# One transfer of 96 rows on partitions 16 to 111, in place of two of 48 rows on partitions 0 to 95

## The chip, the cores and the metric

The kernel runs on one core of one Trainium2 chip. The metric is the device time of one execution in microseconds. The kernel before takes 3562.27 us (median of three runs, 3552.61 to 3563.42). The profile that is read below is of one more execution, which took 3547.51 us.

## The reference, cut to what matters

The input x has one image, 48 channels and 256 x 256 pixels in 32-bit floats (12.58 MB). Two layers follow one another, each adding its result to its input.

```python
# group norm: 16 groups of 3 channels, mean and variance over the whole image
x = x + conv_attention(gn(x))     # layer 0
x = x + window_mix(gn(x))         # layer 1

def conv_attention(x):            # w_qkv (144,48), w_dw (144,1,3,3), w_proj (48,48)
    qkv = dwconv3x3(einsum('bchw,oc->bohw', x, w_qkv), w_dw)
    q, k, v = heads(unfold(split(qkv)))     # 8 heads, 4x4 patches, padded by one border of patches
    attn = softmax(einsum('bhcn,bhcm->bhnm', l2norm(q), l2norm(k)) * temperature)
    return einsum('bchw,oc->bohw', fold(einsum('bhcn,bhnm->bhcm', v, attn)), w_proj)

def window_mix(x):                # 64 x 64 windows, three terms
    return einsum('bcphqw,twW,thH,tcC->bCpHqW', windows(x), Ws, Hs, Cs)
```

The change touches the first group norm, the output projection `w_proj` with the residual that follows it, and the second group norm.

## The kernel before, in words

The image is handled as two halves of 128 rows. A tile that holds "both halves" has 96 partitions: the 48 channels of the upper half on partitions 0 to 47, the 48 channels of the lower half on partitions 48 to 95. So one matmul with a block-diagonal weight (`wq`, `wp`) works on both halves. DRAM keeps x as channel, row, column, and each half of a tile is brought in by a transfer of its own with 48 rows.

**Constants** (L84 to L131). Small weights are loaded from GpSimd's queue (POOL), one after another: `tb` (L89), the group matrix `gm` (L91), twelve pieces of weights into `wq`, `wr` and `wp` (L104, L108), and 21 pieces of the depthwise weights into `dwt` (L114). That makes 35 transfers. [...]the ninth waits until the first has landed, and so on.

**First norm** (L417 to L446). POOL clears a small tile `zr` (L421), whose rows serve as the zero rows above and below an intermediate image in DRAM (L424). x is read whole into `xr`, ten blocks of rows, the upper half from SyncE's queue (SP) and the lower from ScalarE's (L432). VectorE (DVE) takes statistics of two rows at a time (`bn_stats`, L436, 64 of them), joins them (`bn_aggr`, L133), and `group_stats` forms each group's mean and 1/std by two matmuls with `gm`. The result scales `wq` and `wr`, and a copy of `wr` goes to partitions 64 to 111 by a transfer (L441).

**Pointwise and depthwise stages, attention**. From the resident `xr` TensorE forms q, k, v of the first two heads (L155), and the depthwise filter of the first head follows (`depthwise_first`). The attention over eight heads (L674 and on, an order written out by hand) takes most of the time. Its last head also loads the first three tiles `xt0` to `xt2` of x (L756, 24 transfers of 192 KB) for the residual, and stores its results to `os_` in DRAM (L645). `os_` has 16 blocks of 256 patches; `store` puts patches of the upper half into blocks 0 to 7, those of the lower half into blocks 8 to 15.

**Projection and residual** (L787 to L828). Eight steps. Each brings 96 rows of attention results (`pot`, two transfers of 768 KB, L798) and, from the fourth step on, 96 rows of x (`pxt`, the same size, L800), both with three buffers; TensorE multiplies by `wp` (16 matmuls, L812), DVE adds onto the x tile (four adds, L819) and takes statistics (eight, L823), and POOL stores the tile to `x1s` in DRAM (two transfers, L828). SP also brings the first pieces of the next stage (`lxq`, L785). Then the second norm is finished by a chain of small steps (L133 to L149, L863 to L876), and the last stage (L941 to L1002) reads `x1s`.

Except in blocks marked `manual_schedule`, the order on each engine comes from the framework's planner: it takes, of the instructions that it holds to be ready, the one that was written first.

Of the kernel before, what the change touches and what calls it, by code (L numbers as in the profile page):

```python
# [9 lines left out]
F32 = mybir.dt.float32  # L10
F32R = mybir.dt.float32r
AF = mybir.ActivationFunctionType
# [5 lines left out]
C = 48  # L18
H = W = 256
HALF = H // 2  # L20
P2 = 2 * C
KS = 4
KK = KS * KS
NH = 8
HD = C * KK // NH
NT = (H // KS) * (W // KS)
NBORDER = (H // KS + 2) * (W // KS + 2) - NT
EPS = 1e-5
# [8 lines left out]
M0 = H0 * HC  # L37
# [4 lines left out]
TP = 256  # L42
# [5 lines left out]
def conv_preact_kernel(  # L48
# [15 lines left out]
    nc = tc.nc  # L64
    xc = x.rearrange("b c y x -> (b c) y x")
    oc = out.rearrange("b c y x -> (b c) y x")

    const = ctx.enter_context(tc.tile_pool(name="const", bufs=1))
# [11 lines left out]
    os_ = dram.tile([NT // TP, C * KK, TP], F32, name="os_")  # L80
    x1s = dram.tile([C, H, W], F32, name="x1s")


    ident = const.tile([128, 128], F32, name="ident")  # L84
    make_identity(nc, ident)
    ones = const.tile([C, 128], F32, name="ones")
# [3 lines left out]
    gm = const.tile([P2, P2], F32, name="gm")  # L90
    nc.gpsimd.dma_start(out=gm, in_=gmat)  # L91
# [3 lines left out]
    wq = const.tile([P2, 2 * M0], F32, name="wq")  # L95
    nc.vector.memset(wq, 0.0)
    wr = const.tile([64 + C, M1], F32, name="wr")
    wp = const.tile([P2, P2], F32, name="wp")
    nc.vector.memset(wp, 0.0)
    for s in range(2):  # L100
        r = slice(s * C, (s + 1) * C)
        for h in range(NH if s == 0 else H0):
            o = s * M0 + h * HC if h < H0 else (h - H0) * HC
            nc.gpsimd.dma_start(  # L104
                out=(wq[r] if h < H0 else wr[0:C])[:, o : o + HC].rearrange("c (z e) -> c z e", z=3),
                in_=w_qkvT.rearrange("c (z h e) -> h c z e", z=3, h=NH)[h],
            )
        nc.gpsimd.dma_start(out=wp[r, r], in_=w_projT)  # L108
    dwt = const.tile([NP1, NH, 9], F32, name="dwt")
    dws = w_dw.rearrange("(z h e) i a b -> z e h (i a b)", z=3, h=NH)  # L110
    for z in range(3):
        for j in range(CH):
            p = (z * CH + j) * 6
# [3 lines left out]

    mean0 = const.tile([P2, 1], F32, name="mean0")
    rstd0 = const.tile([P2, 1], F32, name="rstd0")
    mean1 = const.tile([P2, 1], F32, name="mean1")  # L120
    rstd1 = const.tile([P2, 1], F32, name="rstd1")
# [8 lines left out]
    def group_stats(st, mean, rstd, pool, pspool, behind=lambda: None):  # L130

        mv = pool.tile([P2, 2], F32, name="mv")
        nc.vector.bn_aggr(mv, st.rearrange("p n s -> p (n s)"))  # L133
        pm = pspool.tile([P2, 1], F32, name="pm", tag="pstat")
        nc.tensor.matmul(pm, lhsT=gm, rhs=mv[:, 0:1], start=True, stop=True)
        behind()
        nc.vector.tensor_copy(mean, pm)
        d = pool.tile([P2, 1], F32, name="gsd")
        nc.vector.tensor_sub(d, mv[:, 0:1], mean)
        e = pool.tile([P2, 1], F32, name="gse")  # L140
        nc.vector.scalar_tensor_tensor(e, d, d, mv[:, 1:2], ALU.mult, ALU.add)
        pv = pspool.tile([P2, 1], F32, name="pv", tag="pstat")
        nc.tensor.matmul(pv, lhsT=gm, rhs=e, start=True, stop=True)
        behind()
        f = pool.tile([P2, 1], F32, name="gsf")
        nc.vector.tensor_scalar_add(f, pv, EPS)
        g = pool.tile([P2, 1], F32, name="gsg")
        nc.scalar.activation(g, f, AF.Sqrt)  # L148
        nc.vector.reciprocal(rstd, g)  # L149
        return mv, e  # L150
# [166 lines left out]
    NM = NT // 512  # L317
# [99 lines left out]
    with tc.tile_pool(name="xn", bufs=1) as xnp, tc.tile_pool(name="cst", bufs=1) as cst, tc.tile_pool(  # L417
# [7 lines left out]
        xr = xnp.tile([P2, HALF, W], F32, name="xr")  # L425
        parts = [16] * 7 + [8, 4, 4]
        st0 = cst.tile([P2, HALF * W // 512, 6], F32, name="st0")
        for i, LR in enumerate(parts):
            j = sum(parts[:i])
            for s in range(2):  # L430
                eng = nc.sync if s == 0 else nc.scalar
                eng.dma_start(  # L432
                    out=xr[s * C : (s + 1) * C, j : j + LR, :], in_=xc[:, s * HALF + j : s * HALF + j + LR, :]
                )
            for i in range(0, LR, 2):
                nc.vector.bn_stats(st0[:, (j + i) // 2, :], xr[:, j + i : j + i + 2, :].rearrange("p a b -> p (a b)"))  # L436
        group_stats(st0, mean0, rstd0, cst, nps)

        nc.vector.tensor_scalar_mul(wq, wq, rstd0)
        nc.vector.tensor_scalar_mul(wr[0:C], wr[0:C], rstd0[0:C])  # L440
        nc.gpsimd.dma_start(out=wr[64 : 64 + C], in_=wr[0:C])  # L441
        for g, (w, k) in enumerate(((wq, P2), (wr, C))):
            m = w.shape[1]
            pb = nps.tile([128, 1], F32, name="pb0", tag="pstat")
            nc.tensor.matmul(pb[:m], lhsT=w[:k], rhs=mean0[:k], start=True, stop=True)
            nc.vector.tensor_scalar_mul(bias[:m, g : g + 1], pb[:m], -1.0)  # L446
# [31 lines left out]
        for i in range(NH + 1):  # L478
            nc.tensor.matmul(pr[:, i : i + 1], lhsT=row[:, i, :], rhs=ones[0:1, 0:1], start=True, stop=True)
# [63 lines left out]
    with tc.tile_pool(name="ahead", bufs=2) as ah, tc.tile_pool(name="ae", bufs=3) as ae, tc.tile_pool(  # L543
# [94 lines left out]
        def store(h, pair):  # L638

            T = 512 // TP  # L640
            for u in range(2):
                m, last, j = parts_of(2 * pair + u)
                for p0, p1, n, c in ((0, HD, m, 0), (HD, 128, last, j * 32)):
                    rows = os_[n * T : (n + 1) * T, h * HD + c : h * HD + c + p1 - p0, :]
                    nc.gpsimd.dma_start(  # L645
                        out=rows.rearrange("t c n -> c t n"),
                        in_=oaccs[h, pair][p0:p1, u, :].rearrange("c (t n) -> c t n", t=T),
                    )
# [14 lines left out]
        with tc.manual_schedule():  # L663
            load_query(0, 1)
            block = scores(0, 0)
            for h in range(NH):
                more = h + 1 < NH
                rows = {r: Depthwise(h + 1, r) for r in range(CR + 1)} if more else {}
                for g in range(NG):
                    p, d, n = rows.get(g - 2), rows.get(g - 1), rows.get(g)  # L670

                    if not more and g == 0:
                        convolution.close()
                        early = ExitStack()  # L674
                        pe = early.enter_context(tc.tile_pool(name="pe", bufs=1, side="right"))
                        xts = [pe.tile([P2, RP, W], F32, name=f"xt{t}") for t in range(NX)]
# [55 lines left out]
                    for k in range(NK):  # L732
# [18 lines left out]
                        if not more and 0 < g <= 2 * NX and k in (1, 3):  # L751
                            i = (g - 1) * 2 + k // 2
                            t, y = i // 4, i % 4 * (RP // 4)
                            for half in range(2):
                                y0 = half * HALF + t * RP + y
                                nc.sync.dma_start(  # L756
                                    out=xts[t][half * C : (half + 1) * C, y : y + RP // 4, :],
                                    in_=xc[:, y0 : y0 + RP // 4, :],
                                )
# [27 lines left out]
    with tc.tile_pool(name="pj", bufs=3) as pj, tc.tile_pool(name="pjs", bufs=1) as pjs, tc.tile_pool(  # L787
        name="pps", bufs=3, space=PSUM
    ) as pps, tc.tile_pool(name="pp1", bufs=1, space=PSUM) as pp1:
        st1 = pjs.tile([P2, HALF * W // 512, 6], F32, name="st1")  # L790
        ov = os_.rearrange("t (c k) n -> t c k n", k=KK)
        for t in range(HALF // RP):
            ot = pj.tile([P2, KK, NP], F32, name="pot")
            xt = xts[t] if t < NX else pj.tile([P2, RP, W], F32, name="pxt")
            for s in range(2):
                r = slice(s * C, (s + 1) * C)
                y0 = s * HALF + t * RP
                nc.sync.dma_start(out=ot[r], in_=ov[s * (NT // 2 // TP) + t])  # L798
                if t >= NX:
                    nc.sync.dma_start(out=xt[r], in_=xc[:, y0 : y0 + RP, :])  # L800
# [3 lines left out]
            for part in range(np):  # L804
# [3 lines left out]
                for ki in range(KS):  # L808
                    ps = pps.tile([P2, KS, n], F32, name="pps")
# [16 lines left out]
                for s in range(2):  # L826
                    y0 = s * HALF + t * RP + ys.start
                    nc.gpsimd.dma_start(out=x1s[:, y0 : y0 + R, :], in_=xt[s * C : (s + 1) * C, ys])  # L828
# [10 lines left out]
        at = pjs.tile([C, 64 + CK], F32, name="at")  # L839
# [3 lines left out]
        gm2 = pjs.tile([P2, 64 + CK], F32, name="gm2")  # L843
        nc.vector.memset(gm2, 0.0)
        for o in (0, 64):
            nc.vector.tensor_copy(gm2[:, o : o + C], gm[:, 0:C])
        busy = pps.tile([P2, KS, 128], F32, name="pps")

        def occupy(rhs):

            n = rhs.free_size()
            nc.tensor.matmul(  # L852
                busy.rearrange("p k n -> p (k n)")[:, :n], lhsT=ident[: rhs.shape[0], :P2], rhs=rhs, start=True, stop=True
            )

        with tc.manual_schedule(engines={mybir.EngineType.PE}):
# [5 lines left out]
            pc1 = pp1.tile([64 + CK, 1], F32, name="pc1", tag="pstat")  # L862
            nc.tensor.matmul(pc1, lhsT=gm2, rhs=e1, start=True, stop=True)  # L863
            occupy(nmx)
            rstd2 = pjs.tile([64 + CK, 1], F32, name="rstd2")
# [4 lines left out]
            nc.vector.tensor_scalar_mul(csn[: 64 + CK], csn[: 64 + CK], rstd2)  # L870
            mcol = pjs.tile([C, 64 + CK], F32, name="mcol")
            nc.vector.tensor_scalar_mul(mcol, at, mean1[0:C])
            pb1 = pp1.tile([64 + CK, T3 * C], F32, name="pb1")
            nc.tensor.matmul(pb1, lhsT=mcol, rhs=csn[0:C], start=True, stop=True)  # L874
# [200 lines left out]
```

## Time and profile before

| | us |
|---|---|
| profiled execution, its own time | 3547.51 |
| its span (first to last instruction) | 3545.7 |
| median of three runs | 3562.27 |
| x load and first norm, to the first pointwise matmul | 0 to 72.7 |
| pointwise matmuls | 72.7 to 131.7 |
| depthwise stage and attention, to the last weighing matmul | 131.7 to 3161.5 |
| projection, from its first load to the joining of statistics | 3165.5 to 3300.8 |
| end of the second norm | 3307.5 |
| last stage | 3307.8 to the end |

The span is the time from the first to the last instruction of one execution. Engines are PE (TensorE), DVE (VectorE), ACT (ScalarE), POOL (GpSimd) and SP (SyncE). A timeline row has start, duration, engine, line, operation and tiles, and in brackets the idle time before it and what ended that. A row of groups has the total busy time, the mean of one in ns, then the idle time before them and what ended it. A row of stretches has, for each engine, busy time and number of instructions; then the TensorE clock granted, the busy share of the 16 DMA engines and their rate.

### The profile page before, as it was taken

The numbers are of one execution on the slowest core, as the hardware profiler recorded it, in microseconds if no ns is written. First come the engines' busy times: TensorE is split into PE (matmuls) and PEld (weight loads), VectorE is DVE, ScalarE is ACT, GpSimd is POOL, SyncE is SP. The second block draws the span as 40 slices with busy tenths as digits, with TensorE's granted clock in tenths as the row PEclk, the third lists the DMA queues.
The fourth block names the chain that finished last, engine by engine and source line by source line (L and its number), as shares of the span: only waits on it lengthen the run. The fifth ranks groups of instructions, "written<-read, shape, count | busy, mean of one in ns | idle before, by whom it ended". The sixth has DMA issues, their size and how long they took to land. (4 is left out here: it accounts for less than half of the span.)

```text
span 3545.7 us, 63152 instructions
## 1 busy us (share of the span) xinstructions
PE 3339.1 (94%) x25836; PEld 1859.1 (52%) x25836; DVE 1990.7 (56%) x2983; ACT 1900.0 (54%) x2890; POOL 562.6 (16%) x648
## 2 busy tenths in 40 slices
PE   2878999999999999999999999999999999985898
PEld 1334455555555555555555555555555555531576
DVE  5463675168726872687268727862786222238543
ACT  0245677557645664666467646764676444420343
POOL 2030112012201220122012211221122100000123
PEclk9998999999999999999999999999999999997999
DMA  7455666633332333333233323332333221039764
GB/s 161 165 116 155 164 171 170 178 108 93 83 84 84 95 90 79 86 96 92 78 87 95 88 79 86 96 88 78 85 94 93 75 54 37 19 73 281 204 168 108
DMA packets 229730, 384.13 MB, mean 108 GB/s; under 512 B 77058, under 2 KB 174706, under 8 KB 224920
## 3 DMA queue, kind: packets, MB, share of 16 engines
q1 hardware_dynamic: 191158, 264.95, 27.4%
q0 software_dynamic: 34784, 106.40, 13.3%
q10 hardware_dynamic: 3490, 8.64, 1.1%
q8 instruction: 207, 3.39, 0.4%
q14 instruction: 91, 0.75, 0.1%
HBM read 234.76 MB, written 144.90 MB: 107 GB/s over the span
## 5 line engine op out<-in xcount | busy, mean ns | idle before, releaser
L588 ACT ACTIVATE e<-big,nmx 128x1024 f32<-128x1024 f32 x1024 | 1144.7, 1118 | 907.0 <-PE big L351 889.1
L351 PE MATMUL big<-kt,qt 128*128 128x512 f32 x6144 | 1457.3, 394 | 31.2 <-DMA kt<-qkv 26.2
L622 PE MATMUL big<-e,vn 128*32 128x512 f32 x12288 | 1348.4, 593 | 1.0 <-DVE vn L606 1.0
L351 PEld LDWEIGHTS big<-kt,qt 128*128 128x128 f32 x6144 | 1141.3, 188 | 370.8 <-issue 121.1
L636 DVE TENSOR_TENSOR oacc<-big,oacc 128x1024 f32<-128x1024 f32 x359 | 438.3, 1221 | 760.8 <-PE big L622 760.8
L622 PEld LDWEIGHTS big<-e,vn 128*32 128x32 f32 x12288 | 384.5, 110 | 881.9 <-issue 815.8
L239 DVE SCALAR_TENSOR_TENSOR acc<-pad,dwt,acc 126x1024 f32<-126x1024 f32 x592 | 765.6, 1293 | 33.8 <-ACT acc L220 18.1
L309 POOL DMA_DIRECT2D qkv<-o x72 | 53.0, 737 | 1331.9 <-ACT o L293 1331.9
L303 POOL TENSOR_TENSOR ol<-o,oh 126x1024 fp32r<-126x1024 f32 x78 | 185.3, 2376 | 271.6 <-DVE ss L254 198.6
L602 DVE TENSOR_REDUCE zt<-zs 128x1 f32<-128x5 f32 x256 | 38.7, 151 | 327.1 <-ACT e L588 291.3
L588 ACT ACTIVATION_READ_ACCUMULATOR e<-big,nmx 128x1 f32 x1024 | 196.0, 191 | 0.0
L293 ACT COPY o<-acc 126x1024 f32<-126x1024 f32 x74 | 161.6, 2184 | 0.0
L812 PE MATMUL pps<-pot,wp 96*96 96x512 f32 x128 | 77.0, 765 | 58.7 <-DMA pot<-os__70 46.0
L972 ACT COPY lyt<-pb 128x1024 f32<-128x1024 f32 x69 | 69.9, 1012 | 111.0 <-PE pb L965 108.4
L191 ACT ACTIVATE ot<-big,bias 108x1024 f32<-108x1024 f32 x64 | 68.1, 1112 | 105.8 <-PE big L184 68.5
L220 ACT ACTIVATE acc<-pad,dwt 126x1024 f32<-126x1024 f32 x74 | 84.0, 1135 | 75.9 <-DMA pad<-t 67.8
L148 ACT ACT_TABLE_LOAD x2 | 2.6, 1283 | 204.5 <-DMA x1s<-pxt 153.2
L250 ACT ACTIVATE sq<-acc 126x1024 f32<-126x1024 f32 x74 | 78.4, 1059 | 60.0 <-DVE acc L239 49.1
L228 PE MATMUL dps<-pad,diag 126*126 126x512 f32 x216 | 96.0, 604 | 15.4 <-DMA pad<-t 15.4
L325 POOL DMA_DIRECT2D kt<-qkv x44 | 23.0, 543 | 516.5 <-PE big L351 504.3
L951 DVE COPY lzt<-pa 128x864 f32<-128x864 f32 (+1 forms) x69 | 67.4, 1000 | 59.7 <-PE pa L941 59.7
L254 DVE TENSOR_REDUCE ss<-sq 126x64 f32<-126x1024 f32 x80 | 97.3, 1218 | 6.2 <-ACT sq L250 6.2
(142 smaller groups left out, 1964.5 us busy)
## 6 DMA issues: line engine op xcount, KB each, us to landing
pad<-t SPq DMA_DIRECT2D x238, 254.0 KB
t<-ot SPq DMA_DIRECT2D x64, 435.4 KB
qkv<-ol POOLq DMA_DIRECT2D x78, 336.0 KB, 6.5
qkv<-oh POOLq DMA_DIRECT2D x70, 336.0 KB, 5.7
qt<-qkv SPq DMA_DIRECT2D x176, 96.0 KB
xs<-in_x_dram SPq DMA_DIRECT2D x64, 192.0 KB
pot<-os__70 SPq DMA_DIRECT2D x16, 768.0 KB
out_dram<-lrt POOLq DMA_DIRECT2D x96, 128.0 KB, 3.8
```

Source lines behind the costliest of these rows:

```text
L220: nc.scalar.mul(self.acc, self.pad[:, 0:KS, 0:W], dwt[:, self.h, 0:1])
L228: nc.tensor.matmul(ps[:, i, :], lhsT=diag[:, tap, :], rhs=self.pad[:, y : y + 2, dx : dx + W], start=(tap == 0), stop=(tap == 8),)
L239: nc.vector.scalar_tensor_tensor(self.acc, self.pad[:, dy : dy + KS, dx : dx + W], dwt[:, self.h, tap : tap + 1], self.acc, ALU.mult, ALU.add,
L250: nc.scalar.activation(self.sq, self.acc, AF.Square)
L254: nc.vector.tensor_reduce(self.ss, self.sq.rearrange("p a (x b) -> p x a b", b=KS), AX.XY, ALU.add)
L293: nc.scalar.copy(self.o.rearrange("p (a b) x -> p a b x", a=KS), self.acc.rearrange("p a (x b) -> p a b x", b=KS))
L303: eng.tensor_sub(self.ol, self.o, self.oh.bitcast(F32))
L351: nc.tensor.matmul(ps[:, i, :], lhsT=qt[:, r, q0 : q0 + 128], rhs=kts[2 * j + i][:, r // 2, :], start=(r == 0), stop=(r == 2),)
L588: nc.scalar.activation(e[:, j * 1024 : (j + 1) * 1024], ps.rearrange("p a b -> p (a b)"), AF.Exp, bias=nmx[:, b : b + 1], accum_out=zs[:, ...
L622: nc.tensor.matmul(ps[p * 32 : (p + 1) * 32, u, :], lhsT=vn[:, c * 32 : (c + 1) * 32], rhs=e[:, n * 512 : (n + 1) * 512], start=(i == 0), ...
L636: nc.vector.tensor_add(oaccs[h, pair], ps, old)
L812: nc.tensor.matmul(ps[:, i : i + step, :], lhsT=wp, rhs=ot[:, ki * KS + i : ki * KS + i + step, part * n : (part + 1) * n], start=True, st ...
```

## The change

The tiles of the two halves get 112 partitions. Partition 16 + 2c + s holds channel c of half s; partitions 0 to 15 hold zeros. As x is stored channel, row, column, the rows "channel, half" are then evenly spaced in DRAM, and one transfer brings all 96. This holds for `xr`, `xt`, `pot`, `pxt` and the stores to `x1s`; the blocks of `os_` are renumbered so that the two halves of one step are neighbours.

The zeros are written by ScalarE in `xr` (ten copies of a zero from `zr`, one for each block of rows), and by POOL in the other tiles (nine clearings of 16 partitions by 4096 values: three in the last head, six at the start of the projection; `pot` and `pxt` become six tiles that are used in turn).

Weights and constants follow: `gm`, `wq`, `wp` are laid out for the new order (two small transfers for the group matrix in place of one, and copies on DVE), `gm2` moves to the start, the copy of `wr` to partitions 64 to 111 is made before the norm and both copies are scaled after it, for which two more small matmuls (`pc0`) and a second square root stand behind the first norm. The second norm gets one more small matmul (`pd1`).

```diff
+OFF = 16
+PF = OFF + P2
+    xh = x.rearrange("b c (s y) x -> (b c s) y x", s=2)
...
-    gm = const.tile([P2, P2], F32, name="gm")
-    nc.gpsimd.dma_start(out=gm, in_=gmat)
+    gm = const.tile([PF, PF], F32, name="gm")
...
+    for s in range(2):
+        nc.gpsimd.dma_start(
+            out=gt[OFF + s :: 2], in_=gmat.rearrange("(u c) (v d) -> u c v d", u=2, v=2)[s]
+        )
+    nc.vector.tensor_copy(gm[:, OFF:].rearrange("p (c s) -> p s c", s=2), gt)
...
-        nc.gpsimd.dma_start(out=wp[r, r], in_=w_projT)
+        nc.gpsimd.dma_start(out=wt[OFF + s * C : OFF + (s + 1) * C, s], in_=w_projT)
+    nc.gpsimd.dma_start(out=wr[64 : 64 + C], in_=wr[0:C])
+    nc.vector.tensor_copy(wp[:, OFF:].rearrange("p (c s) -> p s c", s=2), wt)
...
+        hole = zr[:OFF, 0:1].rearrange("p (u v) -> p u v", u=1)
         for i, LR in enumerate(parts):
             j = sum(parts[:i])
-            for s in range(2):
-                eng = nc.sync if s == 0 else nc.scalar
-                eng.dma_start(
-                    out=xr[s * C : (s + 1) * C, j : j + LR, :], in_=xc[:, s * HALF + j : s * HALF + j + LR, :]
-                )
+            nc.scalar.copy(xr[:OFF, j : j + LR, :], hole.to_broadcast([OFF, LR, W]))
+            nc.sync.dma_start(out=xr[OFF:, j : j + LR, :], in_=xh[:, j : j + LR, :])
...
+        nc.tensor.matmul(pc0, lhsT=gm2, rhs=mv0[:, 0:1], start=True, stop=True)
+        nc.vector.tensor_copy(means, pc0)
...
+        nc.tensor.matmul(pc0, lhsT=gm2, rhs=e0, start=True, stop=True)
+        nc.vector.tensor_scalar_add(rstds, pc0, EPS)
+        nc.scalar.activation(rstds, rstds, AF.Sqrt)
+        nc.vector.reciprocal(rstds, rstds)
 
         nc.vector.tensor_scalar_mul(wq, wq, rstd0)
-        nc.vector.tensor_scalar_mul(wr[0:C], wr[0:C], rstd0[0:C])
-        nc.gpsimd.dma_start(out=wr[64 : 64 + C], in_=wr[0:C])
+        for o in (0, 64):
+            nc.vector.tensor_scalar_mul(wr[o : o + C], wr[o : o + C], rstds[o : o + C])
...
+                    n, v = n % (NM // 2), n // (NM // 2)
+                    rows = os_.rearrange("(t v) c n -> v t c n", v=2)[v]
...
+                        for t in xts:
+                            nc.gpsimd.memset(t[:OFF], 0.0)
...
-                            for half in range(2):
-                                y0 = half * HALF + t * RP + y
-                                nc.sync.dma_start(
-                                    out=xts[t][half * C : (half + 1) * C, y : y + RP // 4, :],
-                                    in_=xc[:, y0 : y0 + RP // 4, :],
-                                )
+                            y0 = t * RP + y
+                            nc.sync.dma_start(
+                                out=xts[t][OFF:, y : y + RP // 4, :], in_=xh[:, y0 : y0 + RP // 4, :]
+                            )
...
+        pots = [pj.tile([PF, KK, NP], F32, name=f"pot{t}") for t in range(3)]
+        xus = xts + [pj.tile([PF, RP, W], F32, name=f"pxt{t}") for t in range(3)]
+        for t in pots + xus[NX:]:
+            nc.gpsimd.memset(t[:OFF], 0.0)
         for t in range(HALF // RP):
-            ot = pj.tile([P2, KK, NP], F32, name="pot")
-            xt = xts[t] if t < NX else pj.tile([P2, RP, W], F32, name="pxt")
-            for s in range(2):
-                r = slice(s * C, (s + 1) * C)
-                y0 = s * HALF + t * RP
-                nc.sync.dma_start(out=ot[r], in_=ov[s * (NT // 2 // TP) + t])
-                if t >= NX:
-                    nc.sync.dma_start(out=xt[r], in_=xc[:, y0 : y0 + RP, :])
+            ot = pots[t % 3]
+            xt = xus[t if t < NX else NX + (t - NX) % 3]
+            nc.sync.dma_start(out=ot[OFF:], in_=ov[t])
+            if t >= NX:
+                nc.sync.dma_start(out=xt[OFF:], in_=xh[:, t * RP : (t + 1) * RP, :])
...
-                for s in range(2):
-                    y0 = s * HALF + t * RP + ys.start
-                    nc.gpsimd.dma_start(out=x1s[:, y0 : y0 + R, :], in_=xt[s * C : (s + 1) * C, ys])
+                y0 = t * RP + ys.start
+                nc.gpsimd.dma_start(out=x1h[:, y0 : y0 + R, :], in_=xt[OFF:, ys])
...
+            nc.tensor.matmul(pd1, lhsT=gm2, rhs=mv1[:, 0:1], start=True, stop=True)
+            mcol = pjs.tile([64 + C, 64 + CK], F32, name="mcol")
+            nc.vector.tensor_scalar_mul(mcol, at, pd1)
```

## The prediction

> **What bounds the kernel now.** I read the page first, its busy times and slices.
>
> ```profile
> PE 3339.1 (94%) x25836; PEld 1859.1 (52%) x25836; DVE 1990.7 (56%) x2983; ACT 1900.0 (54%) x2890; POOL 562.6 (16%) x648
> ...
> DMA  7455666633332333333233323332333221039764
> GB/s 161 165 116 155 164 171 170 178 108 93 83 84 84 95 90 79 86 96 92 78 87 95 88 79 86 96 88 78 85 94 93 75 54 37 19 73 281 204 168 108
> ```
>
> TensorE is busy nearly all the time, except in the first slice and in slices 35 to 37: the load of x with the first norm, and the projection. The change works in these two; in the attention between them the tiles of x are loaded under matmuls. So I asked for stretches of both stages, the timeline of POOL and DVE, DVE's waits in the projection, and groups that give prices. The stretches:
>
> ```profile
> 6.00:55.00 49.00, 4.77 (x20) 4.40 (x20) 30.03 (x65) 1.28 (x1) 6.63 (x12) 1.00 1.00 205
> ...
> 3166.00:3198.00 32.00, 15.67 (x30) 5.70 (x31) 16.44 (x18) 0.00 (x0) 1.90 (x7) 0.71 1.02 187
> 3198.00:3240.00 42.00, 30.33 (x51) 9.90 (x49) 39.47 (x38) 0.00 (x0) 3.02 (x6) 0.74 1.00 299
> 3240.00:3300.00 60.00, 33.78 (x52) 11.16 (x53) 43.99 (x49) 0.00 (x0) 5.03 (x10) 0.67 1.00 279
> ```
>
> In all four the DMA share (last but one) is full, while the rate (last) differs: 205 GB/s with pairs of 48-row loads from two queues, 187 where almost only such loads run, 279 to 299 with stores among them. [...] The timeline of POOL at the start:
>
> ```profile
> 2.34 0.59 POOL L91 DMA_DIRECT2D gm<-in_gmat_dram  x1
> ...
> 12.05 0.58 POOL L104 DMA_DIRECT2D wr<-in_w_qkvT_dram  x1 [5.68 <-DMA tb<-in_temp_dram]
> 17.48 0.58 POOL L104 DMA_DIRECT2D wr<-in_w_qkvT_dram  x1 [4.85 <-DMA gm<-in_gmat_dram]
> ...
> 58.89 0.56 POOL L114 DMA_DIRECT2D dwt<-in_w_dw_dram  x1 [2.64 <-DMA wq<-in_w_qkvT_dram]
> ...
> 63.21 6.12 POOL L114 DMA_DIRECT2D dwt<-in_w_dw_dram  x11 [0.21 <-issue]
> 69.31 0.33 POOL L421 MEMSET zr<- 128x258 f32 x1
> ```
>
> The small loads wait for each other's landing while the x load fills the DMA engines. `zr`, which needs nothing, is cleared only after all 35, at 69.31, for the planner takes what was written first. Today that is harmless, as only DRAM's zero rows need it. DVE's timeline then gives the end of the stage:
>
> ```profile
> 58.33 9.59 DVE L436 BATCH_NORM_STATS2 st<-xr 96x6 f32<-96x512 f32 x16 [2.62 <-DMA xr<-in_x_dram]
> 67.95 1.89 DVE L133 BATCH_NORM_AGGREGATE mv<-st 96x2 f32<-96x384 f32 x1
> ```
>
> Last, groups (statistics, ScalarE at two lengths, projection adds) and DVE's waits in the projection:
>
> ```profile
> L436 DVE BATCH_NORM_STATS2 st<-xr 96x6 f32<-96x512 f32 x64 | 38.6, 672 | 12.6 <-DMA xr<-in_x_dram 12.6
> L161 ACT ACTIVATE ot<-pw,bias 72x512 f32<-72x512 f32 x32 | 21.9, 684 | 37.7 <-PE pw L155 37.7
> L191 ACT ACTIVATE ot<-big,bias 108x1024 f32<-108x1024 f32 x64 | 68.1, 1112 | 105.8 <-PE big L184 68.5 <-issue 37.3
> ```
>
> ```profile
> DVE pxt L819 <- DMA pxt<-in_x_dram: 12.2, 3, 5.1
> DVE pxt L819 <- PE pps L812: 6.2, 4, 4.5
> ```
>
> [...]POOL's small loads advance by one in 3.90 us (12.05 to 58.89, 12 steps).
>
> **First stage.** *Load.* One unit (two halves, 16 rows each, 1.57 MB) takes 1.57 MB / 205 GB/s = 7.7 us. [...]I take 6.5, ends 4.8 and 7.7. Eight units end at about 54 us instead of 62. Alone this would be a gain of some 8 us.
>
> *The zeros.* Each statistic reads all 112 partitions, so it waits for ScalarE's copy of its block, and the copy for `zr` on POOL. The small loads become 37 (two for the group matrix, one for the copy of `wr`; 35 + 1 + 1), all written before `zr` and ready early. [...]With one stream [...]the pace is 1.65 us. The first landed at 11.7 us; [...]I put it at 6. The 37th waits for the 29th: 6 + 28 x 1.65 = 52. If the 21 loads of `dwt` (six rows each) go at their price of issue, 0.57 us, from the 15th landing on (6 + 14 x 1.65 = 29), it is 41. I take 46 for `zr`, with ends 36 and 56 from the two ends of the unit.
>
> *From there.* Clearing 0.33. First copy: ScalarE's rows give (1112 - 684) / 512 = 0.84 ns a value, so 16 x 256 values take 1.11 + 3072 x 0.00084 = 3.7 us. All ten make some 30 us, less than the 38.6 us of the 64 statistics, which come to wait for DVE itself: 46 + 0.3 + 3.7 + 38.6 = 88.6 instead of 67.95, **20.7 us later**. Of today's 38.6 us of statistics all but the last 9.6 hide under the load; that cover is gone. Queued behind the waiting statistics are the whole norm, `wq`, and so all pointwise matmuls.
>
> *After the statistics*: two small matmuls, one square root, three short DVE steps and one more scaling stand beside the chain from 67.95 to 72.7; DVE steps of 0.15 to 0.27 us on the path cost 0.5 (0.2 to 1). The copy of `wr` (L441) was off the path. Pointwise matmuls stream the same 512 columns: no change.
>
> **Attention.** Twelve issues on SP go, three clearings on POOL come while POOL idles (327 us before L834). Nothing, under matmuls; without that cover the clearings would cost about 12 us.
>
> **Projection.** DVE needs about 12.55 us a step (four adds at 1.98, eight statistics at 0.68, overlapping slightly), 100.4 in all; it takes 118.9 from 3181.9 to 3300.8, so 18.5 idle, the two waits shown. These are load-bound steps of 14.8 to 18.2 us. The first pair of `pot` takes 12.7 us from issue (3165.5) to matmul (3178.2); a pair costs 1.57 MB / 187 GB/s = 8.4, and at 6.5 I gain 2. [...]of 11 us of loads in each of four steps I take 10%, 4.5 us. Sum **-6.5**, ends 0 and -20.5 (all waits and the first 2). One transfer instead of two saves 0.4 us of SP issue, under transfers in flight.
>
> *Clearings.* Six on POOL: the rows of `zr` (258 values, 0.33) and `csn` (144, 0.22) give 1 ns a value, 4 us each, 24 us in all. Some may come ahead of the `os_` stores at 3157.8, in the gap from 3152, and delay them by 0 to 4; the rest is covered by `pot`'s transfer and, for the later buffers, by steps 1 to 5. Store of step 1 at 3190.8: clearings from 3166.5 end about then. I take 0.5. The extra `pd1` matmul (0.33) delays the next by 0.3. The 96-row `x1s` stores move the same bytes.
>
> **Sum**: 20.7 + 0.5 - 6.5 + 0.5 + 0.3 = **+15.5 us**, against the profiled 3547.5: 3563. The median of the runs lies 14.8 above that execution; against it, 3562.3 + 15.5 = **3578 us**.
>
> **Rivals.** (A) *Zeros in time*: the planner puts `zr` before the small loads, or holds these to be unready. Against it: the same planner kept `zr` behind all 35, though POOL stood waiting for 47 us. Then the load ends the stage at about 58, gain 10; with 6.5 in the projection and 1.3 of additions the time is 3547. It decides from a `zr` at about 20 us. (B) *Late but cheap*: the small loads go at issue price throughout (37 x 0.57 = 21 us, then `zr` near 30), or [...]a unit near 4.8 and all 20.5 us gained later: +4 - 6 or +11 - 19, within 10 us of before, 3552 to 3573. [...] (C) *Copies dearer*: ScalarE's copy with 16-byte steps (L293) took 2.18 us for 1024 values; a repeated zero at that price takes 70 us and passes DVE: 30 us more, 3608. Against it: nothing is strided here.
>
> **Chances.** Forecast 0.50 (its own range 3573 to 3594), A 0.20, B 0.22, C 0.08. Slower by over 0.3% (10.7 us, what a measurement of this kernel can tell) in forecast and C: 0.58; same in B: 0.20, and 0.02 of B with A: faster 0.22. The range 3541 to 3596 leaves out half of A and C.
>
> **What would show it.** Right: `zr` cleared at 36 to 56 us, then `hole` copies with statistics behind them; `bn_aggr` near 89; the stretch of the load above 205 GB/s; DVE's idle in the projection below 18.5. Wrong: `zr` ahead of the `dwt` loads; copies of over 5 us; a rate that stays at 205, which would put `zr` later; in the projection a wait for clearings, or stores of `os_` behind them.

## The result: slower by half a percent, as two large terms partly cancel

Over 20 runs each on one chip, the changed kernel takes 3575.76 us (3562.93 to 3585.58) and the kernel before 3558.53 us (3549.78 to 3571.7): a ratio of 1.0045, with a 95% interval from 1.0033 to 1.0057. The profiled execution of the changed kernel took 3573.81 us, its span is 3571.9 us.

On the page of the changed kernel, the busy times and the slices (as before, DMA share and rate in 40 equal slices):

```profile
PE 3346.9 (94%) x25842; PEld 1868.6 (52%) x25842; DVE 1994.7 (56%) x2992; ACT 1929.1 (54%) x2902; POOL 589.3 (16%) x649
...
DMA  6345666643332333233333333333233321029764
GB/s 146 113 131 136 172 165 170 169 147 88 87 90 78 95 86 87 76 94 87 84 87 96 83 85 87 95 79 87 83 94 92 77 59 45 21 54 311 194 169 103
```

The sums are almost those of before. ScalarE has gained 29 us and GpSimd 27 (copies and clearings of zeros), which says nothing yet of the end. Slice 37 moves 311 GB/s where it was 281. So the stages have to be measured one by one. The table takes each boundary from the timelines: the joining of the first statistics (`bn_aggr`), the first pointwise matmul, the first and last matmul of the attention, the first add of the projection, the joining of the second statistics, the first matmul of the last stage.

| stretch (us) | before | after | difference |
|---|---|---|---|
| start to joining of the first statistics | 67.95 | 101.98 | +34.0 |
| joining to first pointwise matmul | 4.8 | 5.4 | +0.6 |
| pointwise and depthwise work, to the attention | 198.3 | 200.2 | +1.9 |
| attention | 2890.5 | 2891.7 | +1.2 |
| last attention matmul to first projection add | 20.3 | 18.1 | -2.2 |
| projection, first add to second joining | 118.9 | 101.8 | -17.1 |
| second joining to first matmul of the last stage | 7.0 | 8.9 | +1.9 |
| last stage | 237.9 | 243.8 | +5.9 |

The stretches on which the change should act (all but the third, fourth and last) add up to +34.0 + 0.6 - 2.2 - 17.1 + 1.9 = +17.2 us, as much as the two medians differ; from one profile of each kernel, so close an agreement is in part chance. The two profiled executions lie 26.2 us apart; the other 9 us are in the three stretches that the change should leave alone. There the runs scatter: over the profiles of the eleven experiments below, the three together took 3326.6 to 3344.4 us, and both 3326.7 before and 3335.7 after lie within that. So these 9 us are not put down to the change.

**First stage.** GpSimd's timeline of the changed kernel (start, duration, line and operation, how many together, and in brackets the idle time before and what ended it):

```profile
10.50 0.58 POOL L122 DMA_DIRECT2D wr<-in_w_qkvT_dram  x1 [4.22 <-DMA tb<-in_temp_dram]
...
31.74 0.51 POOL L127 DMA_DIRECT2D wr<-wr  x1 [7.92 <-DMA wr<-in_w_qkvT_dram]
...
37.23 0.56 POOL L135 DMA_DIRECT2D dwt<-in_w_dw_dram  x1 [1.95 <-DMA wq<-in_w_qkvT_dram]
...
59.32 0.56 POOL L135 DMA_DIRECT2D dwt<-in_w_dw_dram  x1 [1.12 <-DMA dwt<-in_w_dw_dram]
59.88 0.33 POOL L442 MEMSET zr<- 128x258 f32 x1
```

`zr` is cleared behind all 37 small loads, at 59.88 us. Then ScalarE's and VectorE's timelines:

```profile
60.24 28.32 ACT L452 COPY xr<-zr 16x4096 f32<-16x4096 f32 x10 [58.23 <-POOL zr L442]
```

```profile
38.49 0.21 DVE L128 COPY wp<-wt 112x96 f32<-112x96 f32 x1 [20.70 <-DMA wt<-in_w_projT_dram]
63.88 38.07 DVE L455 BATCH_NORM_STATS2 st<-xr 112x6 f32<-112x512 f32 x64 [25.18 <-ACT xr L452]
101.98 1.89 DVE L154 BATCH_NORM_AGGREGATE mv<-st 112x2 f32<-112x384 f32 x1
```

The chain is complete in four lines: clearing at 59.88, first copy at 60.24, first statistic at 63.88, all 64 without a gap in 38.07 us. ScalarE needs only 28.32 us for ten copies and stays ahead. Keep the first of VectorE's three lines in mind: the small copy of `wp` waited for its load until 38.49. Here that costs nothing.

**Load and projection.** Stretches (start and end, length, busy time and instructions of PE, PEld, DVE, ACT and POOL, then granted clock, DMA share and GB/s):

```profile
6.00:55.00 49.00, 4.78 (x20) 4.40 (x20) 2.83 (x23) 0.00 (x0) 13.58 (x25) 1.00 1.01 226
...
3204.00:3236.00 32.00, 18.28 (x33) 7.11 (x34) 18.46 (x15) 0.00 (x0) 21.51 (x8) 0.72 1.01 271
3236.00:3280.00 44.00, 33.71 (x60) 12.45 (x59) 43.95 (x46) 0.00 (x0) 2.38 (x7) 0.82 0.99 338
```

The load of x runs at 226 GB/s instead of 205 and the projection at up to 338 instead of 299, at the same full DMA share. In the second of these projection stretches VectorE is busy 43.95 of 44 us: it has become the bound of the projection. Of its waits for the loads, 12.2 us before, this is left:

```profile
DVE pxt L852 <- DMA pxt<-in_x_dram: 2.0, 1, 2.0
```

The first add and the joining of the second statistics, before and then after, give the projection's 118.9 and 101.8 us:

```profile
3181.89 4.09 DVE L819 TENSOR_TENSOR xt<-pps,xt 96x1024 f32<-96x1024 f32 x2 [15.34 <-PE pps L812]
3300.78 1.89 DVE L133 BATCH_NORM_AGGREGATE mv<-st 96x2 f32<-96x384 f32 x1
```

```profile
3217.37 4.07 DVE L852 TENSOR_TENSOR xt<-pps,xt 112x1024 f32<-112x1024 f32 x2 [13.63 <-issue]
3319.20 1.89 DVE L154 BATCH_NORM_AGGREGATE mv<-st 112x2 f32<-112x384 f32 x1
```

### The profile page after: what moved, and what is told of

It is laid out like the page before. It is cut to its first block, busy times and chain, and to the rows that moved or that the text cites. A ratio compares the mean times of both kernels' runs of the same rounds, so it can differ in the third digit from the quotient of the medians.

```text
span 3571.9 us, 63147 instructions
## 1 busy us (share of the span) xinstructions
PE 3346.9 (94%) x25842; PEld 1868.6 (52%) x25842; DVE 1994.7 (56%) x2992; ACT 1929.1 (54%) x2902; POOL 589.3 (16%) x649
## 4 chain that ended last, share of the span: by engine, by line
PE 84%; DMA 4%; issue 2%; DVE 1%; SPq 1%; ACT 0%; POOL 0%; POOLq 0%; ACTq 0%; DVEq 0%
PE big L372 39%; PE big L651 36%; PE pb L995 2%; PE pa L971 2%; DMA xs<-in_x_dram 2%; PE pc L1014 2%; PE big L205 1%; DMA pxt<-in_x_dram 1%; PE pst L599 1%; SPq L346 1%; DMA kt<-qkv 0%; PE pn L279 0%; DMA pot<-os__70 0%; DVE xt L852 0%; PE pps L845 0%
## 5 line engine op out<-in xcount | busy, mean ns | idle before, releaser
L260 DVE SCALAR_TENSOR_TENSOR acc<-pad,dwt,acc 126x1024 f32<-126x1024 f32 x592 | 765.6, 1293 | 35.1 <-ACT acc L241 19.3
L845 PE MATMUL pps<-pot,wp 112*112 112x512 f32 x128 | 77.0, 767 | 38.8 <-DVE pxt L852 16.7
L995 PE MATMUL pb<-wsb,lzt 64*64 64x64 f32 x4608 | 89.5, 221 | 10.5 <-issue 7.9
```

The source lines that it names most:

```text
L260: nc.vector.scalar_tensor_tensor(self.acc, self.pad[:, dy : dy + KS, dx : dx + W], dwt[:, self.h, tap : tap + 1], self.acc, ALU.mult, ALU.add,
L995: nc.tensor.matmul(pb[s * WS : (s + 1) * WS, w, n * WS : (n + 1) * WS], lhsT=zts[u][r, t * C + b * 24 + q * 8 + s * 4 + i, :], rhs=wsb[r, ...
```

## The experiments

All eleven compute the complete result. "Theory" and "rival" are told in the expectation of each run. Ratios are against the kernel before, timed on the same chip in the same session.

### e1: the zeros first

```diff
+    zh = const.tile([OFF, 1, 1], F32, name="zh")
+    nc.vector.memset(zh, 0.0)
     ones = ...
-        hole = zr[:OFF, 0:1].rearrange("p (u v) -> p u v", u=1)
+        hole = zh
```

> The changed kernel, but the zero that ScalarE copies lies in a small tile of its own, cleared by VectorE as its first instruction. Theory (the wait for the zero is the loss): the ten copies run from about 2 us, the statistics follow the landing blocks of x, which the changed kernel's trace has at 220 GB/s (57 us), and the joining of statistics starts near 61 us instead of 101.98; the time falls by 41 us from 3575.8 to about 3535, ratio to before 0.993. Rival (the copies or the 112-row statistics themselves are slow, whenever they start): the joining starts no earlier than 90 us, ratio at or above 1.001.

Measured: 3546.29 us against 3557.43, ratio 0.9962 (0.9947 to 0.9976). So the place of one clearing decides the sign: the ratio falls from 1.0045 to 0.9962, some 30 us. The joining moves from 101.98 to 70.72, 31 us. But 70.72 is no earlier than before the change (67.95), though x arrives faster. VectorE's timeline of this run says why:

```profile
39.61 0.21 DVE L130 COPY wp<-wt 112x96 f32<-112x96 f32 x1 [15.61 <-DMA wt<-in_w_projT_dram]
39.74 30.95 DVE L457 BATCH_NORM_STATS2 st<-xr 112x6 f32<-112x512 f32 x52
70.72 1.89 DVE L156 BATCH_NORM_AGGREGATE mv<-st 112x2 f32<-112x384 f32 x1
```

Twelve statistics run early; then VectorE stands 15.61 us at the copy of `wp`, whose small load comes late through GpSimd's queue, and 52 statistics follow in one row. The zero was hiding a second wait of the same kind.

### e2: the zeros in the middle of the small loads

```diff
+    zh = const.tile([OFF, 1, 1], F32, name="zh")
+    nc.gpsimd.memset(zh, 0.0)
     dwt = const.tile([NP1, NH, 9], F32, name="dwt")
-        hole = zr[:OFF, 0:1].rearrange("p (u v) -> p u v", u=1)
+        hole = zh
```

> The changed kernel, but the zero lies in a tile of its own that GpSimd clears after the weights and the copy of wr, before the 21 depthwise loads (near 32.3 us in the changed kernel's trace instead of 59.88). Theory: the end of the first stage follows the zero at a fixed distance, 3.7 us to the first statistic and 38.1 us of statistics, so the joining starts near 74 us and the time is about 28 us below the change, 3548, ratio to before 0.997. Rival (something else holds the stage, such as the landing of x): the same end as with the zeros first, near 61 us, or no gain.

Measured: 3549.85 us, ratio 0.9982 (0.9972 to 0.9992). The zero was there at 33.23 us, and its copy some 3.7 us later would have started the statistics near 37. They started with the copy of `wp`, and all 64 behind it:

```profile
39.63 0.21 DVE L128 COPY wp<-wt 112x96 f32<-112x96 f32 x1 [21.86 <-DMA wt<-in_w_projT_dram]
39.76 38.07 DVE L457 BATCH_NORM_STATS2 st<-xr 112x6 f32<-112x512 f32 x64
77.86 1.89 DVE L156 BATCH_NORM_AGGREGATE mv<-st 112x2 f32<-112x384 f32 x1
```

Three places of the zero give joinings of 70.72, 77.86 and 101.98. From the start of the statistics on, the rule of the prediction holds: start + 38.1.

### e3: no zeros at all, rows 0 to 95

Theory A is that the placement on rows 16 to 111 makes the loads faster, theory B that the single transfer of 96 rows does.

```diff
-OFF = 16
+OFF = 0
-            nc.scalar.copy(xr[:OFF, j : j + LR, :], hole.to_broadcast([OFF, LR, W]))
...
-                        for t in xts:
-                            nc.gpsimd.memset(t[:OFF], 0.0)
...
-        for t in pots + xus[NX:]:
-            nc.gpsimd.memset(t[:OFF], 0.0)
```

> The changed kernel with its 96 rows on partitions 0 to 95: halves still alternate and one transfer still brings them, but there are no zero rows, no copies and no clearings. Theory A [...]: [...]x loads at 205 GB/s or less, the joining starts near 68 us, the idle time of VectorE in the projection is back at 12 to 18 us, and the time is about 3558, ratio to before 1.000. Theory B (one transfer [...]is what helps, wherever it lies): x at 220 GB/s or more, idle near 2 us, about 3535, ratio 0.993.

Measured: 3545.75 us, ratio 0.996 (0.9946 to 0.9975), the same as e1. Here rows 0 to 95 are one transfer, without the shift by 16. The loads of x at the start, first in e3 and then in e1:

```profile
6.00:55.00 49.00, 4.77 (x20) 4.40 (x20) 25.20 (x61) 0.00 (x0) 12.51 (x23) 1.00 1.01 221
```

```profile
6.00:55.00 49.00, 4.77 (x20) 4.40 (x20) 25.03 (x61) 25.64 (x10) 13.04 (x24) 1.00 1.00 223
```

The rates are 221 and 223 GB/s, the projections 103.2 and 102.8 us, the joinings 70.55 and 70.72. So the shift to row 16 does not make the loads faster at this size (16 KB for each partition), and the ten copies of zeros, 25.64 us of ScalarE in that stretch, cost nothing once the zero is early. What e1 and e3 share against the kernel before is the alternating order of the halves, one queue for the first load in place of two, and the transfer of all 96 rows at once. The next run takes away the last of these alone.

### e4: the same tiles, each transfer cut between row 63 and row 64

Here theory A is that the placement of the tile decides, theory B that each transfer by itself has to span all 96 rows. On top of e1, loads and `x1s` stores alike:

```diff
-            nc.sync.dma_start(out=xr[OFF:, j : j + LR, :], in_=xh[:, j : j + LR, :])
+            for p in (0, C):
+                nc.sync.dma_start(out=xr[OFF + p : OFF + p + C, j : j + LR, :], in_=xh[p : p + C, j : j + LR, :])
```

> The kernel with the zeros first and the same placement on 16 to 111, but each transfer of 96 rows is cut in two of 48, rows 16 to 63 and 64 to 111, loads and stores alike. Theory A [...]: as with the zeros first, 0.993. Theory B [...]: loads at 190 to 205 GB/s, the joining starts near 66 us, idle time of 12 us or more in the projection, about 3555, ratio 0.999.

Measured: 3593.34 us, ratio 1.0115 (1.0086 to 1.0143). The stretch of the load, and VectorE's wait in the projection (total, times, longest):

```profile
6.00:55.00 49.00, 4.77 (x20) 4.39 (x20) 6.27 (x29) 25.64 (x10) 8.79 (x16) 1.00 1.02 142
```

```profile
DVE pxt L857 <- DMA pxt<-in_x_dram: 26.8, 3, 9.5
```

142 GB/s at a full share: the transfer of rows 16 to 63, and then of 64 to 111, is far slower than both in one (223) and slower than before's two of rows 0 to 47 and 48 to 95 (205). At the start before's two came from two queues; in the projection all of them come from SyncE in both kernels, and there too 134.7 us stand against 118.9. Neither theory had forecast as much: the rate lies far below the 190 to 205 of theory B. With equal tiles, the two transfers reach 142 GB/s where one reaches 223. They also are twice as many and half as large, which e7 takes up below.

### e5 and e6: the copy of `wp` away from VectorE

e5 is e1, and e6 is e3, each with

```diff
-    nc.vector.tensor_copy(wp[:, OFF:].rearrange("p (c s) -> p s c", s=2), wt)
+    nc.gpsimd.tensor_copy(wp[:, OFF:].rearrange("p (c s) -> p s c", s=2), wt)
```

> The kernel with the zeros first (run with 0.9962), and besides the copy that forms wp from its small load moved from VectorE to GpSimd. Theory: with the zeros first this copy, which stood on VectorE between two statistics until its load had landed at 39.7 us, was what kept the joining of statistics at 70.72; without it the statistics follow the x load (223 GB/s, last block near 57 us) and the joining starts near 60 us, about 10 us below that run: 3536, ratio to before 0.993. Rival (the landing of x holds the end of the statistics): no change, joining near 70 us, ratio 0.996.

> Rows 0 to 95 with one transfer (run with 0.996), with the same copy moved to GpSimd. If zeros and placement cost and bring nothing by themselves: like the same edit on 16 to 111, joining near 60 us, about 3536, ratio 0.993. If the balanced placement on 16 to 111 loads faster once nothing else holds VectorE: joining 3 us or more later than there.

Measured: e5 3533.54 us against 3558.81, ratio 0.993 (0.9913 to 0.9947); e6 3539.4, ratio 0.9941 (0.9924 to 0.9959). VectorE's timeline of e5:

```profile
52.44 9.59 DVE L457 BATCH_NORM_STATS2 st<-xr 112x6 f32<-112x512 f32 x16 [2.22 <-DMA xr<-in_x_dram]
62.07 1.89 DVE L156 BATCH_NORM_AGGREGATE mv<-st 112x2 f32<-112x384 f32 x1
```

The statistics wait for x again, as before the change, and the joining is at 62.07 (e6: 63.08), 8.7 and 7.5 us earlier than with the copy on VectorE. That shows the second wait. Now the faster load itself counts. In the stretch from 6 to 50 us, e5 loads at 228 GB/s and e6 at 222, against 203 in the kernel before:

```profile
6.00:50.00 44.00, 4.77 (x20) 4.40 (x20) 25.90 (x58) 0.00 (x0) 6.06 (x11) 1.00 1.00 203
```

### e7, e9 and e10: all rows in one transfer, but shorter runs

e7 is e5 with the loads of x in the first stage and of `pot` and `pxt` in the projection, and every `x1s` store, cut in two along the values of a partition (for x, along the image rows), so that each partition gets 8 KB in one run instead of 16. e9 cuts e7's loads once more, to 4 KB. e10 is e6 cut as e7; its first case is that the placement on rows 16 to 111 counts once the runs are short, its second that it does not. The theory of e9 is that still shorter runs load still faster.

```diff
-            nc.sync.dma_start(out=xr[OFF:, j : j + LR, :], in_=xh[:, j : j + LR, :])
+            for y in (j, j + LR // 2):
+                nc.sync.dma_start(out=xr[OFF:, y : y + LR // 2, :], in_=xh[:, y : y + LR // 2, :])
```

> The kernel with the zeros first and the copy off VectorE, rows 16 to 111, each transfer cut in two, but each of the two covers all 96 rows and half of each row's values (8 KB runs in place of 16 KB). Theory (what counts is that a transfer spans all the rows at once, not how many transfers there are): x at 215 GB/s or more, VectorE's projection 104 us or less from first add to joining, about 3538, ratio 0.994. Rival (fewer and larger transfers are what helps): x at 205 or less, that part of the projection at 110 us or more, ratio 0.998 or above.

> As the run with each transfer cut in two along the values of a row (0.9909, x at 258 GB/s), but the loads of x, pot and pxt cut in four: 4 KB runs. Theory [...]: x at 270 GB/s or more; VectorE then sets the first stage (first statistic near 14.9 us plus 38.6), joining near 53.5 us, projection loop already at VectorE's 99.7 us, so 3523 to 3526, ratio 0.990 to 0.991. Rival (two transfers in flight were the cause[...]): x below 250, joining at 57 us or more, ratio 0.992 or above.

> Rows 0 to 95, copy off VectorE, each transfer cut in two along the values of a row (8 KB runs). [...]x below 245 GB/s, joining 2 us or more after the 54.79 of the same edit on 16 to 111, ratio 0.993 or above. If it does not[...]: x near 258, joining near 55 us, ratio 0.991.

Measured: e7 3525.63 us, ratio 0.9909 (0.9889 to 0.9928); e9 3522.41 against 3560.3, ratio 0.9908 (0.9872 to 0.9943); e10 3529.83, ratio 0.9919 (0.99 to 0.9938). The stretches of the load in e5, e7, e9 and e10, in this order:

```profile
6.00:50.00 44.00, 4.78 (x20) 4.40 (x20) 31.08 (x70) 25.64 (x10) 11.81 (x22) 1.00 1.02 228
```

```profile
6.00:50.00 44.00, 4.78 (x20) 4.40 (x20) 35.95 (x79) 25.63 (x10) 19.87 (x44) 1.00 1.03 258
```

```profile
6.00:50.00 44.00, 4.78 (x20) 4.40 (x20) 38.21 (x82) 25.63 (x10) 19.65 (x44) 1.00 1.05 266
```

```profile
6.00:50.00 44.00, 4.78 (x20) 4.40 (x20) 33.69 (x74) 0.00 (x0) 19.72 (x44) 1.00 1.04 243
```

Twice as many transfers are faster where each spans all 96 rows: 228, 258, 266 GB/s for runs of 16, 8 and 4 KB. The expectation of e7 had only asked whether the rate would hold; the gain is the finding. So e4 was not slow because it had twice as many transfers. The joining falls from 62.07 to 54.79 and 52.91, the time from the last attention matmul to the first projection add from 18.2 to 14.0 and 12.7. From 8 to 4 KB the total no longer moves (0.9909 and 0.9908). The small loads profit as well: `zr`, still behind all of them, was cleared at 59.98 us in e5 and at 40.98 in e7. With 8 KB runs the shift to rows 16 to 111 is ahead of rows 0 to 95 by 258 to 243 GB/s and by 2.6 us of joining (54.79 against 57.40); with 16 KB it was 228 to 222 and 1.0 us. So in e10 the rate and the joining came as forecast for the case in which the placement counts, but its ratio, 0.9919, lies between the two cases, and the intervals of the ratios overlap. From one profile of each kernel, that is a small effect of the placement at most.

### e8: two queues

e6 with the blocks of x taken in turn by SyncE's and ScalarE's queues:

```diff
-            nc.sync.dma_start(out=xr[OFF:, j : j + LR, :], in_=xh[:, j : j + LR, :])
+            (nc.sync if i % 2 == 0 else nc.scalar).dma_start(out=xr[OFF:, j : j + LR, :], in_=xh[:, j : j + LR, :])
```

> Rows 0 to 95 with the copy off VectorE, blocks of x issued in turn from SP and ACT, each still one transfer of 96 rows. If one queue limits the x load, the rate goes above 240 GB/s and the joining starts near 55 us, ratio 0.992; [...]the rate stays at 205 to 225 and the joining near 60 us, ratio 0.993 to 0.994. The small loads of GpSimd then[...] slow down.

Measured: 3544.82 us, ratio 0.9963 (0.995 to 0.9976), and 215 GB/s against 222 with one queue. Two blocks are now under way at a time and land together, so VectorE gets its work in pairs:

```profile
48.61 9.59 DVE L453 BATCH_NORM_STATS2 st<-xr 96x6 f32<-96x512 f32 x16 [5.62 <-DMA xr<-in_x_dram]
...
59.67 9.59 DVE L453 BATCH_NORM_STATS2 st<-xr 96x6 f32<-96x512 f32 x16 [1.48 <-DMA xr<-in_x_dram]
```

The joining goes from 63.08 to 69.37, though near 60 was forecast for the case of an unchanged rate. The second queue brought nothing to the rate and took the order away.

### e11: the kernel before, with shorter runs

Each of before's 48-row loads and stores cut in two along the image rows, nothing else:

```diff
-                eng.dma_start(
-                    out=xr[s * C : (s + 1) * C, j : j + LR, :], in_=xc[:, s * HALF + j : s * HALF + j + LR, :]
-                )
+                for y in (j, j + LR // 2):
+                    eng.dma_start(
+                        out=xr[s * C : (s + 1) * C, y : y + LR // 2, :],
+                        in_=xc[:, s * HALF + y : s * HALF + y + LR // 2, :],
+                    )
```

> The kernel before, halves on 0 to 47 and 48 to 95, every load of x, pot and pxt and every store to x1s cut in two along the values of a row, so four transfers of 8 KB runs in place of two of 16 KB. If short runs alone are what helps: x at 240 GB/s or more, joining near 58 us, projection loop below 108 us, ratio 0.994 or below. If a transfer has to span all 96 rows: x at 190 to 215 GB/s, joining at 65 to 72 us, loop at 115 us or more, ratio 0.998 to 1.004.

Measured: 3536.79 us, ratio 0.9935 (0.9915 to 0.9955): 219 GB/s instead of 203, joining at 61.46 instead of 67.95, projection 115.8 instead of 118.9.

```profile
6.00:50.00 44.00, 4.77 (x20) 4.40 (x20) 30.68 (x66) 0.00 (x0) 12.82 (x23) 1.00 1.03 219
```

The stages lie between the two forecasts. So shorter runs help without the change too, but in the projection they don't replace the transfer over all rows (99.7 in e7). In the total this advantage of e7 is not clear: its interval, 0.9889 to 0.9928, overlaps that of e11, 0.9915 to 0.9955. The stretches on which the edit should act account for 12 of the 23 us that e11 gains; where the rest comes from was not found.

## Why the prediction was right, and where its steps were not

The sum, +15.5 us, came out at +17.2, and the sign and the main mechanism were right: the zeros arrive behind GpSimd's small loads and lay the statistics bare. Two of its terms, though, were wrong by 13 us each, in opposite directions. That the total came so close is luck.

**Zeros, term "I take 46 for `zr`": mis-sized, measured 59.88.** The pace was good: from the ninth small load, one of `wr`, at 10.50 to the last `dwt` load at 59.32 the queue made 28 steps of 1.74 us, against the 1.65 that I had estimated, and that no trace had shown. What failed was the start and the second case mixed into the 46. The first landing came at 10.2 us, not at 6. And the `dwt` loads did not go at their price of issue: from 37.23 to 59.32 they took 1.47 us a step, and before them the copy of `wr` held the queue for 7.92 us. Had I taken 10.2 and the measured pace for all, 10.2 + 28 x 1.74 = 58.9. The upper end that I gave, 56, was too low.

**From the clearing to the joining: right.** Predicted 0.3 + 3.7 + 38.6 = 42.6 us, measured 101.98 - 59.88 = 42.1; first copy 3.64 us, ten copies 28.32 against "some 30". Together, +34.0 instead of +20.7. e1 and e2, which move the zero alone, show that this term is what makes the kernel slower.

**Load unit, 6.5 us: a little short.** 1.57 MB at 226 GB/s are 7.0 us, within the ends of 4.8 and 7.7. The 6.5 and the lower end of 4.8 us were estimates of mine that no trace had shown, and the 4.8 were reached by no run; the fastest, e9 at 266 GB/s, needs 5.9. In the changed kernel this gain is invisible, for VectorE, once it has its zeros, waits for no block of x; e5 shows it.

**After the statistics, +0.5: right**, 5.4 instead of 4.8. The pointwise matmuls took 624 ns each on 112 partitions and 620 on 96, as good as the same, as predicted.

**Projection, -6.5: mis-sized, measured -19.3.** The first pair, 2 us, was right (2.2). The failed step is "of 11 us of loads in each of four steps I take 10%". Nearly all of the 18.5 us in which VectorE waited went (17.1), as in the lower end, -20.5. My argument was the rate with stores among the loads, 279 to 299 GB/s against 187 where almost only loads run. e4 shows in its place that the span of the transfers sets this time although stores run among them: 102.8 us in e1, 134.7 in e4.

**Clearings, +0.5: 0.** Those of the projection came behind the last `os_` stores, from 3204.21 on, two groups of three in 10.4 us each (3.5 us a tile, 4 predicted). VectorE waited for none of them, and e3, which has no clearings, took the same 18.1 us from the last attention matmul to the first add.

**After the projection, +0.3: +1.9.** There is one more matmul, and in that window the granted clock was 0.92 before and 0.56 after. In e11, which has the code of before there, the window took 8.1 us against 7.0, so some of this is scatter. It was not separated.

**The rivals.** A, zeros in time, was put at 3547 us, and e1 took 3546.29; but that is a coincidence, for its terms were others. Its joining was to come at 58 and came at 70.7, because of the wait for `wp` that neither forecast nor rival had seen, and the projection gave three times what it counted. Of B, the half with the zero near 30 fell, and its other half is part of what happened: nearly all of the 20.5 us in the projection were gained, though with a unit of 7.0 us and not of 4.8. C, dearer copies, fell with the 28.32 us.

**What stays open.** That spanning all rows raises the rate is shown (142 GB/s in e4, 223 in e1), and so is that cutting the 96-row transfers along the values does (228 in e5, 258 in e7, 266 in e9). The cut makes runs shorter, and transfers smaller and more numerous, all at once; that the length of the run is what counts is not shown by itself. Why either helps is not shown. With the same source and the same tile, the shape of the transfers moved the rate from 142 GB/s (e4) to 266 (e9) at a full DMA share, so a full share does not tell how much is moved; what holds the DMA engines at the lower rates was not measured. A cause on the side of DRAM, where neighbouring rows of a transfer of x lie 128 KiB apart in the new order and 256 KiB in the old, was not tested.

## What to carry to other kernels

When an edit makes one engine wait for a value, look for the instruction that writes it and count what stands ahead of it in that engine's queue: a clearing that took 0.33 us cost 34 us here, and when it was moved up, a copy of 0.21 us behind the same small loads became the next wait. Let each large transfer span all the rows of its tile (223 GB/s here, 142 when it was cut in two), and try shorter runs per partition (258 GB/s with 8 KB, 228 with 16) before concluding that a full DMA share is the limit; together with the two waits removed this gave 0.991 of the time before, from a change that alone made the kernel slower. But try the small edit on the old kernel too: shorter runs alone gave 0.9935 there. A total that agrees with a forecast proves its terms only if they are measured one by one.

## What the runs showed of the hardware

- Loads of x between 6 and 50 us, on rows 16 to 111: with 16 KB runs per partition 228 GB/s (e5), with 8 KB 258 (e7), with 4 KB 266 (e9); on rows 0 to 95, 222 with 16 KB (e6) and 243 with 8 (e10); as two loads of 48 rows from two queues, 203 with 16 KB (before) and 219 with 8 (e11).
- Between 6 and 55 us, the same 96 rows cut between rows 63 and 64 of the tile: 142 GB/s at a full DMA share (e4), against 223 uncut (e1).
- Rows 16 to 111 and 0 to 95 load nearly alike with 16 KB runs: 223 and 221 GB/s in e1 and e3.
- Small loads by GpSimd slow down beside a second queue of large loads: from the ninth to the fifteenth of them, each step took 3.91 us in the kernel before (x on two queues) and 2.13 in the changed kernel (x on one). In e6 (one queue) the first of them had landed at 10.3 us and GpSimd ran 21 instructions between 6 and 50 us; in e8 (two), at 13.0 us, and 8. Shorter runs in the large stream speed them up: `zr`, cleared behind all of them, came at 59.98 us in e5 and at 40.98 in e7.
